# One-hot forms stored once and loaded again, and the count stretch's keys made four columns at a time, in a four-layer graph network

## The chip, the cores and the metric

The kernel runs on one core of one Trainium2 chip. The time is device microseconds of one execution. Before the change it is 6291.43 us, the median of 14 executions (6259.13 to 6341.54).

The core's engines are named as in the profile: PE is TensorE (its weight loads are a row of their own, PEld), DVE is VectorE, ACT is ScalarE, POOL is GpSimd, SP is SyncE, which here issues most of the DMAs. Each engine works through its own instructions in order.

## What is computed

A graph of N = 3125 nodes with 128 features and E = 100,000 edges (`src`, `dst`, sorted by `dst`) goes through four residual blocks, each before a layer norm and a ReLU:

```python
edge_index = jnp.stack([src, dst])
h = jnp.maximum(_layernorm(x, axis=-1), 0.0)
x = x + _L0_gnn_ref(h, edge_index, ...)      # 3 attention layers, one head, with self loops
h = jnp.maximum(_layernorm(x, axis=-1), 0.0)
x = x + _L1_gnn_ref(h, edge_index, edge_attr_64, ...)   # messages by a 3-layer MLP per edge
h = jnp.maximum(_layernorm(x, axis=-1), 0.0)
x = x + _L2_gnn_ref(h, edge_index, ...)      # 2 attention layers with 4 heads
h = jnp.maximum(_layernorm(x, axis=-1), 0.0)
x = x + _L3_gnn_ref(h, edge_index, edge_weight, ...)    # 2 graph convolutions
```

The several-headed layer, which the change touches most, is

```python
e = jax.nn.leaky_relu(xl[src] + xr[dst], NEG)
score = jnp.einsum('ehd,hd->eh', e, att)
m = jax.ops.segment_max(score, dst, num_segments=N)
ex = jnp.exp(score - m[dst])
den = jax.ops.segment_sum(ex, dst, num_segments=N)
alpha = ex / (den[dst] + 1e-16)
out = jax.ops.segment_sum(alpha[:, :, None] * xl[src], dst, num_segments=N)
```

## The kernel before

**Tiles.** Nodes lie in 25 tiles of 128. Edges are sorted by destination, so that the edges of a range of destinations are one range of the list. Two plans cut this list (class `Plan`). The plan for counting has 196 windows of 16 destinations (`cw`), each a matrix of 128 edges by k columns: most windows have 3 or 4 columns (68 and 56 windows), 24 have 5, 16 have 6, 8 each have 7, 8 and 11, 2 have 12, and the first six have 59, 25, 20, 17, 15 and 13; 1025 columns in all. The plan for the edge layers has 30 windows (`ew`) of at most 128 destinations, 840 columns ("chunks" of 128 edges) in all. Chunks are handled in groups of up to C = 4: 15, 11, 8, 9, 10, 8, 7, 7, 12, 10, 9, 9, 8, 8, 7, 7, 7, then 6 seven times... down to 2 groups a window, 220 groups in all.

**Stages in order.**
1. *Count stretch* (`count_edges`). For each of the 196 windows, it counts the edges between sources and destinations by matmuls of one-hot matrices: `by_src` (line 1043, through the helper `even`: the low seven bits of the source against 0..127, for 8 columns at once) is the stationary operand and `by_key` (line 1092, the key against 0..399, one column each) the moving one. The sums go to `count` on ACT.
2. *Three one-headed attention layers* on the dense count matrix.
3. *Message layer* (`message_layer`), over the 220 groups. For each: four gathers of table rows by POOL (line 1348, 128 rows each); a DMA `row` (line 1355) that puts the places of the group's 512 edges within their node tile on all partitions; `at` (line 1359), on DVE, is 1 where partition and place agree (bf16, 128x512); `by_feature` (lines 1371 and 1376) sums node part and gathered part in PSUM; after the MLP, `w` (line 1364), on DVE, is the same relation the other way round (float32, edges on partitions, 512 columns), and line 1577 sums messages by node with it.
4. *Two several-headed layers* (`dynamic_attention_layer`), over the same 30 windows and 220 groups each. `scored` makes the gathers, `row`, `at`, `by_feature`, the leaky ReLU (lines 1806 on ACT and 1807 on DVE), and the scores (line 1813). `weighed` finds the maxima of runs (`run_maxima`, scans on DVE) and the exponentials (line 1831). `summed` makes `w` again (line 1364), `msg` (line 1847) and the sums by node (line 1852). The gathered rows stay in one of G2 = 20 buffers `g2` from `scored` until `summed`. A window's sums are run either beside the next but one window's scores ("apart") or within the next window's ("merged"): `apart = steps(i - 1) + steps(i) + steps(i + 1) < G2`.
   Beside these layers runs `adjacency`, which makes the weighted dense adjacency for the last stage: one-hot matrices by `even` and line 1771, matmuls of line 1775 into one PSUM bank `W`, a copy `rows` by ACT (line 1781) and a DMA to `adj` (line 1782), 196 times.
5. *Two convolutions* on the dense adjacency, read back by DMA.

**Order.** The loops are unrolled in Python; a scheduler then places each engine's instructions, so that work of later groups stands ahead of earlier groups' where buffers allow it. The number of buffers of a tile (`bufs`) says how far: `row` 4, `at` 3, `w` 3, `g1` 6 groups. All plain loads and stores (`row`, `er`, `lane`, `pk`, `adj<-rows`, tables) are issued by SP in its one order; a store waits there until its data is made, and what stands behind it waits too. The gathers are issued by POOL.

**Both layers make the same forms again.** `at` and `w` depend on the edges' places alone, not on the layer. Before the change, they are made by DVE three times: in the message layer and in each several-headed layer.

Of the kernel before, what the change touches and what calls it, by code (L numbers as in the profile page):

```python
# [8 lines left out]
F32 = mybir.dt.float32  # L9
# [735 lines left out]
def sorted_path(ctx: ExitStack, tc: tile.TileContext, a: dict, out: bass.AP, flag_out: bass.AP):  # L745
# [23 lines left out]
    def bc(ap, shape):  # L769
        return ap.to_broadcast(shape)  # L770
# [32 lines left out]
                   allow_small_or_imprecise_dtypes=True)  # L803
    iota_by = const.tile([P, P, 8], BF16, name="iota_by")
    nc.vector.tensor_copy(iota_by, bc(iota_row[:, :, None], [P, P, 8]))
    weights = []

    def load_matrix(name, src):
# [231 lines left out]
    def even(out_t, a_t, row, j0, n, op):  # L1040

        n += n % 2
        nc.vector.tensor_tensor(out_t[:, :, :n], a_t[:, :, :n], bc(row[:, None, j0:j0 + n], [P, P, n]), op)  # L1043

    def count_edges(count):

        with tc.tile_pool(name="f_cw", bufs=2) as wp:
            tail0 = plan.nw * NW
            nc.vector.memset(count[:, :, tail0:], 0)
            many = wp.tile([P, plan.nw], F32, name="many", bufs=1)  # L1050
            below_255 = wp.tile([P, 1], F32, name="below_255", bufs=1)
            nc.vector.memset(below_255, -254.0)
            for w0, w1, c0, cols in plan.batches:
                code = wp.tile([P, cols, 2], I32, name="code", bufs=1)
                own = wp.tile([P, cols], F32, name="own", bufs=1)
                for w, col, k in plan.cw[w0:w1]:
                    r = at_register(base_c, w, P * k)
                    reads.append(nc.sync.dma_start(
                        code[:, col - c0:col - c0 + k, :],
                        codes[bass.ds(r, P * k), :].rearrange("(p k) i -> p k i", p=P)))  # L1060
                    nc.gpsimd.memset(own[:, col - c0:col - c0 + k + k % 2], float(w))
                    if k % 2:
                        nc.gpsimd.memset(code[:, col - c0 + k:col - c0 + k + 1, :], 0)
                ti = wp.tile([P, cols], I32, name="ti", bufs=1)
                tf = wp.tile([P, cols], F32, name="tf", bufs=1)
                keep = wp.tile([P, 3, cols], F32, name="keep", bufs=2)
                key = keep[:, 0, :]
                low = wp.tile([P, cols], BF16, name="low", bufs=2)
                code_i = code[:, :, 0]

                nc.vector.tensor_scalar(ti, code_i, 16, None, ALU.logical_shift_right)
                nc.vector.tensor_tensor(own, ti, own, ALU.not_equal)
                nc.vector.tensor_scalar(ti, code_i, 127, None, ALU.bitwise_and)
                nc.vector.scalar_tensor_tensor(keep[:, 1, :], own, FAR, ti, ALU.mult, ALU.add)
                nc.vector.tensor_copy(low, keep[:, 1, :])

                nc.vector.tensor_scalar(ti, code_i, 12, NW - 1, ALU.logical_shift_right, ALU.bitwise_and)
                nc.vector.tensor_copy(tf, ti)
                nc.vector.tensor_scalar(ti, code_i, 7, 31, ALU.logical_shift_right, ALU.bitwise_and)
                nc.vector.scalar_tensor_tensor(key, ti, float(NW), tf, ALU.mult, ALU.add)  # L1080
                nc.scalar.copy(keep[:, 2, :], code[:, :, 1].bitcast(F32))
                nc.sync.dma_start(kept[:, :, c0:c0 + cols], keep)
                for w, col, k in plan.cw[w0:w1]:
                    pt = bank("ABC"[w % 3])
                    for k0 in range(0, k, 8):
                        kn = min(8, k - k0)
                        j0 = col - c0 + k0
                        by_src = wp.tile([P, P, 8], BF16, name="by_src", bufs=3)
                        even(by_src, iota_by, low, j0, kn, ALU.is_equal)
                        for i in range(kn):  # L1090
                            by_key = wp.tile([P, n_key], BF16, name="by_key", bufs=6)
                            nc.vector.tensor_scalar(by_key, iota_key, key[:, j0 + i:j0 + i + 1], None,  # L1092
                                                    ALU.is_equal)
                            nc.tensor.matmul(pt[:, :n_key], by_src[:, :, i], by_key,  # L1094
                                             start=(k0 + i == 0), stop=(k0 + i == k - 1))
                    nc.scalar.copy(count[:, :, w * NW:(w + 1) * NW],
                                   pt[:, :n_key].rearrange("p (t d) -> p t d", d=NW))
                    junk = wp.tile([P, n_key], BF16, name="junk")
                    nc.scalar.activation(junk, pt[:, :n_key], AF.Relu, bias=below_255,
                                         accum_out=many[:, w:w + 1])  # L1100
            worst = wp.tile([P, 1], F32, name="worst", bufs=1)
            nc.vector.tensor_reduce(worst, many, AX.X, ALU.add)
            pt = bank("D")
            nc.tensor.matmul(pt[:1, :1], worst, ones[:, 0:1], start=True, stop=True)
            nc.vector.tensor_copy(flags[:, 3:4], pt[:1, :1])
            load_edge_windows(wp)
            for t in range(NT):
                own_t = count[:, t, t * P:(t + 1) * P]
                nc.vector.tensor_add(own_t, own_t, ident)
# [236 lines left out]
    def gather(tab, g, j0, c0, n):  # L1346
        for c in reversed(range(n)):
            nc.gpsimd.indirect_dma_start(  # L1348
                out=g[:, j0 + c, :], out_offset=None, in_=tab,
                in_offset=bass.IndirectOffsetOnAxis(ap=src_i[:, c0 + c:c0 + c + 1], axis=0))  # L1350

    def node_by_slot(c0, n):

        row = wk.tile([P, SL], BF16, name="row", bufs=4)
        nc.sync.dma_start(row[:, :n * P], bass.AP(tensor=place_d.tensor,
                                                  offset=place_d.offset + c0 * P,
                                                  ap=[[0, P], [1, n * P]]))
        at = wk.tile([P, SL], BF16, name="at", bufs=3)
        nc.vector.tensor_scalar(at[:, :n * P], row[:, :n * P], pidx, None, ALU.is_equal)  # L1359
        return at  # L1360

    def slot_by_node(c0, n):
        w = wk.tile([P, C, P], F32, name="w", bufs=3)
        nc.vector.tensor_tensor(w[:, :n, :], bc(iota_row[:, None, :], [P, n, P]),  # L1364
                                bc(dst_l[:, c0:c0 + n, None], [P, n, P]), ALU.is_equal)
        return w

    def by_feature(pt, R3, t, at, g, j0, n, more=None):
# [371 lines left out]
    def adjacency(pool):  # L1740
        for t in range(NT):
# [16 lines left out]
            for w, col, k in ws:  # L1758
                sums = bank("W")
                for k0 in range(0, k, C):  # L1760
                    kn = min(C, k - k0)
                    j0 = col - c0 + k0
                    by_src = pool.tile([P, P, C], BF16, name="by_src")
                    even(by_src, iota_by, low, j0, kn, ALU.is_equal)
                    by_wgt = [pool.tile([P, P, C], BF16, name=f"by_wgt{q}") for q in range(3)]
                    for q, part in enumerate((w1, w2, w3)):
                        even(by_wgt[q], by_src, part, j0, kn, ALU.mult)
                    yield
                    by_key = pool.tile([P, C, n_key], BF16, name="by_key")
                    for i in reversed(range(kn)):  # L1770
                        nc.vector.tensor_scalar(by_key[:, i, :], iota_key, pk[:, 0, j0 + i:j0 + i + 1],  # L1771
                                                None, ALU.is_equal)
                    for i in range(kn):
                        for q in range(3):
                            nc.tensor.matmul(sums[:, :n_key], by_wgt[q][:, :, i], by_key[:, i, :],  # L1775
                                             start=(k0 + i + q == 0),
                                             stop=(k0 + i == k - 1 and q == 2))
                    if k0 + kn < k:
                        yield
                rows = pool.tile([P, n_key], F32, name="rows")  # L1780
                nc.scalar.copy(rows, sums[:, :n_key])
                nc.sync.dma_start(adj[t, :, w % per, :], rows)
                yield

    most_cols = max(sum(c[2] + c[2] % 2 for c in plan.cw if c[0] // per == t) for t in range(NT))

    G2 = 20


    def dynamic_attention_layer(i_layer, R3, T3, beside):  # L1790
# [3 lines left out]
        def scored(i, S, gs):  # L1794

            _, _, t, w0, k = plan.ew[i]
            for c0, n in chunks_of(w0, k):
# [1 line left out]
                g = gp.tile([P, C, D], F32, name="g2", bufs=G2)  # L1799
                gs.append(g)  # L1800
                gather(tab, g, 0, c0, n)
                at = node_by_slot(c0, n)
                y1 = bank("A")
                by_feature(y1, R3, t, at, g, 0, n)
                low_y = wk.tile([P, SL], F32, name="low_y", bufs=3)
# [28 lines left out]
        def summed(i, exs, gs):  # L1834
# [6 lines left out]
            for c0, n in chunks_of(w0, k):  # L1841
# [1 line left out]

                msg = wk.tile([P, C * HEADS, HW], F32, name="msg", bufs=3)
                e = ex[:, j0:j0 + n, :].rearrange("p c h -> p (c h)")
                w = slot_by_node(c0, n)
                nc.vector.tensor_mul(msg[:, :n * HEADS, :HD],  # L1847
                                     gs[j0 // C][:, :n, :].rearrange("p c (h d) -> p (c h) d", d=HD),
                                     bc(e[:, :, None], [P, n * HEADS, HD]))
# [171 lines left out]
```

## Time and profile before

| what | value |
|---|---|
| median of 14 executions | 6291.43 us |
| profiled execution, its own time | 6316.27 us |
| its span | 6314.4 us |
| PE busy | 4691.3 us (74%) |
| PE weight loads busy | 3855.0 us (61%) |
| DVE busy | 3396.1 us (54%) |
| ACT busy | 1743.5 us (28%) |
| POOL busy | 2562.6 us (41%) |
| mean granted PE clock | 0.84 |
| moved by DMA | 423.25 MB, 67 GB/s over the span |
| queue of SP's and ACT's DMAs (q1) | 248.15 MB, 13.5% of 16 engines |
| queue of POOL's gathers (q0) | 166.13 MB, 10.7% of 16 engines |

The operations that the change touches, each as a group of the profile:

| line, engine | what | count | busy us | mean ns |
|---|---|---|---|---|
| 1092 DVE | `by_key` of the count stretch, 128x400 | 1025 | 260.1 | 317 |
| 1094 PE | count matmuls, 128x400 | 1025 | 97.7 + 84.6 + 83.7 | 356, 347, 355 |
| 1359 DVE | `at`, 128x512 bf16 | 660 | 230.0 | 349 |
| 1364 DVE | `w`, 128x512 float32 | 660 | 434.9 | 660 |
| 1348 POOL | gathers | 2520 | 2532.8 | 1005 |
| 1781 ACT | `rows` | 196 | 96.4 | 492 |

How to read it: a group's busy time is the union of its instructions' spans, its mean is that of one. Instructions of one engine overlap in the profile by a few tens of nanoseconds and more, so the time that one takes from its engine's stream is read from start to start on the timeline. "Idle before, released by" names the engine whose semaphore came last before the instruction; "issue" is a wait that no semaphore in the profile explains. Some matmul records are missing from a trace.

### The profile page before, as it was taken

The page shows a single profiled execution, that of the slowest core. Times are in us where ns is not written, and L with a number is a line of the kernel's source. Part 1 is how long each engine was busy: PE and PEld are TensorE (multiplying, and loading weights), DVE is VectorE, ACT ScalarE, POOL GpSimd, SP SyncE. Part 2 cuts the span into 40 slices and gives each one's busy share as a digit, 9 for nine tenths or more (in the row PEclk, how much of TensorE's full clock was granted, in tenths as well). Part 3 has the DMA queues.
Part 4 walks back from the last instruction along what each step waited for, and adds up shares of the span by engine and source line. Part 5 has one row for each costly group of instructions (what it writes and reads, how often), then busy time and mean ns, then how long its engine had stood idle before and what let it go on. Part 6 is the DMA issues. An engine that isn't in the chain of part 4 may idle for free. (4 is left out here: it accounts for less than half of the span.)

```text
span 6314.4 us, 85314 instructions
## 1 busy us (share of the span) xinstructions
PE 4691.3 (74%) x30043; PEld 3855.0 (61%) x30361; DVE 3396.1 (54%) x9835; ACT 1743.5 (28%) x4234; POOL 2562.6 (41%) x3155
## 2 busy tenths in 40 slices
PE   4769995878887886567687767874576777677798
PEld 2339984767776775346465656663465555566698
DVE  7998885333334445345455546572354555566633
ACT  1578884222222232111111112121111212122211
POOL 1000001656666563454544445634645454455200
PEclk9989996889999997778787778886787888788899
DMA  1010002333333331122222222221222222222266
GB/s 47 7 22 1 2 1 52 80 82 85 78 86 82 80 82 50 42 53 53 55 57 60 57 59 65 67 55 50 62 67 64 70 70 68 70 74 73 86 250 219
DMA packets 299197, 423.25 MB, mean 67 GB/s; under 512 B 113380, under 2 KB 243090, under 8 KB 292614
## 3 DMA queue, kind: packets, MB, share of 16 engines
q1 hardware_dynamic: 215589, 248.15, 13.5%
q0 software_dynamic: 80800, 166.13, 10.7%
q8 instruction: 241, 3.95, 0.3%
q10 hardware_dynamic: 2368, 3.40, 0.2%
q14 instruction: 199, 1.62, 0.1%
HBM read 367.97 MB, written 49.45 MB: 66 GB/s over the span
## 5 line engine op out<-in xcount | busy, mean ns | idle before, releaser
L1348 POOL DMA_INDIRECT g<-tab,src_i x2520 | 2532.8, 1005 | 3140.3 <-issue 967.7
L1364 DVE TENSOR_TENSOR w<-iota_row,dst_l 128x512 f32<-128x512 f32 (+2 forms) x660 | 434.9, 660 | 854.0 <-remote 271.3
L1775 PE MATMUL W<-by_key,by_wgt 128*128 128x400 bf16 x3075 | 705.1, 376 | 193.8 <-issue 105.0
L1852 PE MATMUL C<-msg,w 128*128 128x132 f32 x3360 | 570.6, 313 | 178.6 <-issue 155.5
L1807 DVE TENSOR_TENSOR low_y<-A,low_y 128x512 f32<-128x512 f32 (+3 forms) x440 | 291.0, 661 | 748.6 <-ACT low_y L1806 416.0
L1376 PEld LDWEIGHTS A<-ident,g 128*128 128x128 f32 x3360 | 502.7, 210 | 293.1 <-issue 220.4
L1376 PE MATMUL A<-ident,g 128*128 128x128 f32 x3360 | 529.8, 295 | 196.7 <-issue 175.9
L1813 PE MATMUL sp<-att_h,low_y 128*128 128x4 f32 x3360 | 463.2, 257 | 262.0 <-issue 144.6
L1813 PEld LDWEIGHTS sp<-att_h,low_y 128*128 128x128 f32 x3360 | 470.3, 212 | 283.0 <-issue 152.4
L1775 PEld LDWEIGHTS <-by_wgt 128*128 128x128 bf16 x3075 | 365.1, 123 | 434.7 <-issue 302.2
L1852 PEld LDWEIGHTS C<-msg,w 128*128 128x128 f32 x3360 | 489.1, 216 | 207.6 <-issue 187.6
L1806 ACT ACTIVATE low_y<-A 128x512 f32<-128x512 f32 (+3 forms) x440 | 254.2, 578 | 1197.8 <-PE A L1376 658.8
L1371 PE MATMUL A<-at,R 128*128 128x512 bf16 (+3 forms) x1108 | 370.3, 402 | 91.3 <-issue 60.8
L1043 DVE TENSOR_TENSOR by_wgt<-by_src,w 128x512 bf16<-128x512 bf16 (+1 forms) x918 | 329.1, 396 | 168.8 <-remote 85.5
L1630 PE MATMUL B<-ets,w1c 128*128 128x256 f32 (+1 forms) x868 | 266.1, 434 | 157.1 <-DVE ets L1619 95.5
L1371 PEld LDWEIGHTS <-R 128*128 128x128 bf16 x1980 | 201.0, 105 | 222.7 <-issue 117.4
L1359 DVE TENSOR_SCALAR at<-row,pidx 128x512 bf16<-128x512 bf16 (+2 forms) x660 | 230.0, 349 | 172.5 <-remote 78.8
L1577 PE MATMUL C<-x,w 128*128 128x130 f32 x1680 | 257.4, 293 | 68.9 <-ACT x L1569 62.9
L1636 ACT ACTIVATE x<-B,mb 128x512 f32<-128x512 f32 (+1 forms) x220 | 146.7, 667 | 572.1 <-PE B L1376 302.7
L1771 DVE TENSOR_SCALAR by_key<-iota_key,pk 128x400 bf16<-128x400 f16 x1025 | 287.1, 323 | 30.8 <-PE A L1376 14.6
L1094 PEld LDWEIGHTS <-by_src 128*128 128x128 bf16 x1025 | 134.0, 149 | 273.6 <-DVE by_key L1092 158.2
L1847 DVE TENSOR_TENSOR msg<-g,ex 128x512 f32<-128x512 f32 (+3 forms) x440 | 286.8, 659 | 7.8 <-ACT ex L1831 5.3
(404 smaller groups left out, 7670.3 us busy)
## 6 DMA issues: line engine op xcount, KB each, us to landing
A<-adj SPq DMA_DIRECT2D x48, 1600.0 KB
row<-place_d SPq DMA_DIRECT2D x597, 128.0 KB
g<-tab,src_i POOLq DMA_INDIRECT x2520
adj<-rows SPq DMA_DIRECT2D x196, 200.0 KB
er<-in_edge_attr_dram SPq DMA_DIRECT2D x39, 512.0 KB
tab<-T SPq DMA_DIRECT2D x21, 192.0 KB
row<-place_d SPq DMA_DIRECT2D x24, 96.0 KB
A<-adj SPq DMA_DIRECT2D x2, 800.0 KB
```

Source lines behind the costliest of these rows:

```text
L1043: nc.vector.tensor_tensor(out_t[:, :, :n], a_t[:, :, :n], bc(row[:, None, j0:j0 + n], [P, P, n]), op)
L1348: nc.gpsimd.indirect_dma_start(out=g[:, j0 + c, :], out_offset=None, in_=tab, in_offset=bass.IndirectOffsetOnAxis(ap=src_i[:, c0 + c:c0 + ...
L1364: nc.vector.tensor_tensor(w[:, :n, :], bc(iota_row[:, None, :], [P, n, P]), bc(dst_l[:, c0:c0 + n, None], [P, n, P]), ALU.is_equal)
L1371: nc.tensor.matmul(pt[:, :n * P], R3[i][:, t * D:(t + 1) * D], at[:, :n * P], start=(i == 0), stop=False, skip_group_check=True)
L1376: nc.tensor.matmul(pt[:, c * P:(c + 1) * P], g[:, j0 + c, :], ident, start=False, stop=(c == n - 1), skip_group_check=True)
L1630: nc.tensor.matmul(p3[:, c:n:2, :], W1c[:, c, :], ets[:, :m * P].rearrange("p (c e) -> p c e", e=P), start=False, stop=False, skip_group_c ...
L1771: nc.vector.tensor_scalar(by_key[:, i, :], iota_key, pk[:, 0, j0 + i:j0 + i + 1], None, ALU.is_equal)
L1775: nc.tensor.matmul(sums[:, :n_key], by_wgt[q][:, :, i], by_key[:, i, :], start=(k0 + i + q == 0), stop=(k0 + i == k - 1 and q == 2))
L1807: nc.vector.tensor_max(low_y[:, :n * P], y1[:, :n * P], low_y[:, :n * P])
L1813: nc.tensor.matmul(sp[:, c * HEADS:(c + 1) * HEADS], low_y[:, c * P:(c + 1) * P], att_h, start=True, stop=True)
L1847: nc.vector.tensor_mul(msg[:, :n * HEADS, :HD], gs[j0 // C][:, :n, :].rearrange("p c (h d) -> p (c h) d", d=HD), bc(e[:, :, None], [P, n * ...
L1852: nc.tensor.matmul(acc[:, :AW], w[:, c, :], msg[:, c * HEADS:(c + 1) * HEADS, :].rearrange("p h d -> p (h d)"), start=(i == first_of[t] an ...
```

## The change

Three things change.

*Count stretch.* Four columns' keys are made by one tensor_tensor of 128 x 400 x 4 through the helper `even`, against an iota repeated four times (`iota_kby`, a new constant) and an f16 copy of the keys (`key16`, made by ACT once for each of the four batches). `even` rounds an odd number of columns up to the next even one. The matmuls read their moving operand with a step of four elements.

```diff
+    iota_kby = const.tile([P, NT * NW, C], F16, name="iota_kby")
+    nc.vector.tensor_copy(iota_kby, bc(iota_key[:, :, None], [P, NT * NW, C]))
...
-        nc.vector.tensor_tensor(out_t[:, :, :n], a_t[:, :, :n], bc(row[:, None, j0:j0 + n], [P, P, n]), op)
+        nc.vector.tensor_tensor(out_t[:, :, :n], a_t[:, :, :n],
+                                bc(row[:, None, j0:j0 + n], [P, a_t.shape[1], n]), op)
...
+                key16 = wp.tile([P, cols], F16, name="key16", bufs=2)
+                nc.scalar.copy(key16, key)
...
-                        for i in range(kn):
-                            by_key = wp.tile([P, n_key], BF16, name="by_key", bufs=6)
-                            nc.vector.tensor_scalar(by_key, iota_key, key[:, j0 + i:j0 + i + 1], None,
-                                                    ALU.is_equal)
-                            nc.tensor.matmul(pt[:, :n_key], by_src[:, :, i], by_key,
-                                             start=(k0 + i == 0), stop=(k0 + i == k - 1))
+                        for i0 in range(0, kn, C):
+                            by_key = wp.tile([P, n_key, C], BF16, name="by_key", bufs=3)
+                            even(by_key, iota_kby, key16, j0 + i0, min(C, kn - i0), ALU.is_equal)
+                            for i in range(i0, min(i0 + C, kn)):
+                                nc.tensor.matmul(pt[:, :n_key], by_src[:, :, i], by_key[:, :, i - i0],
+                                                 start=(k0 + i == 0), stop=(k0 + i == k - 1))
```

*One-hot forms.* The message layer still makes `at` and `w` on DVE, and now also stores each to DRAM. The several-headed layers load them instead of loading `row` and making them: one load of up to 128 KB for `at`, one of up to 256 KB for `w` a group, all issued by SP.

```diff
+    at_d = dram.tile([-(-KT // C) + NE, P, SL], BF16, name="at_d")
+    at_row = {}
+
+    def node_by_slot_again(c0, n):
+        at = wk.tile([P, SL], BF16, name="at", bufs=5)
+        nc.sync.dma_start(at[:, :n * P], at_d[at_row[c0], :, :n * P])
+        return at
...
         nc.vector.tensor_scalar(at[:, :n * P], row[:, :n * P], pidx, None, ALU.is_equal)
+        at_row[c0] = len(at_row)
+        nc.sync.dma_start(at_d[at_row[c0], :, :n * P], at[:, :n * P])
         return at
+
+    w_d = dram.tile([-(-KT // C) + NE, P, C * P], F32, name="w_d")
+
+    def slot_by_node_again(c0, n):
+        w = wk.tile([P, C, P], F32, name="w", bufs=4)
+        nc.sync.dma_start(w[:, :n, :].rearrange("p c d -> p (c d)"), w_d[at_row[c0], :, :n * P])
+        return w
...
+        nc.sync.dma_start(w_d[at_row[c0], :, :n * P], w[:, :n, :].rearrange("p c d -> p (c d)"))
         return w
...
-                at = node_by_slot(c0, n)
+                at = node_by_slot_again(c0, n)
...
-                w = slot_by_node(c0, n)
+                w = slot_by_node_again(c0, n)
```

*Buffers.* `rows` of `adjacency` has one buffer instead of two, and G2 is 19 instead of 20.

```diff
-                rows = pool.tile([P, n_key], F32, name="rows")
+                rows = pool.tile([P, n_key], F32, name="rows", bufs=1)
...
-    G2 = 20
+    G2 = 19
```

## The prediction

> **What bounds the kernel now.** I read first the stretches of the span by stage, since an average over the span mixes four limits. Columns: length of the stretch, then busy time and number of instructions of PE, weight load, DVE, ACT and POOL, then granted clock, DMA share and GB/s.
>
> ```profile
> 60.00:440.00 380.00, 268.97 (x1050) 137.94 (x1050) 369.21 (x1309) 212.56 (x593) 9.38 (x280) 0.96 0.08 11
> ...
> 1010.00:2500.00 1490.00, 1151.99 (x7339) 997.24 (x7446) 582.51 (x1719) 415.54 (x1027) 827.95 (x840) 0.88 0.30 78
> 2490.00:4230.00 1740.00, 1257.80 (x7562) 985.62 (x7668) 929.30 (x2747) 281.93 (x900) 845.41 (x840) 0.79 0.22 57
> 4230.00:5970.00 1740.00, 1210.28 (x7379) 959.51 (x7486) 925.30 (x2835) 330.38 (x1071) 859.40 (x840) 0.78 0.25 65
> ```
>
> The count stretch (first row) is DVE's: 369 of 380 us. In the message layer (second row) and in the two several-headed layers (last two) PE is the busiest by far, and DVE has about half of its time free.
>
> Then two short stretches inside the first several-headed layer:
>
> ```profile
> 2635.00:2665.00 30.00, 29.68 (x216) 23.77 (x219) 23.12 (x70) 6.13 (x16) 0.00 (x0) 1.00 0.12 32
> 3005.00:3032.00 27.00, 9.38 (x23) 3.76 (x23) 1.78 (x4) 0.60 (x1) 17.98 (x20) 0.56 0.22 56
> ```
>
> When the layer runs well, PE is full (29.68 of 30 us) with DVE at 77%. When it runs badly, PE makes 23 matmuls in 27 us, while POOL issues gather after gather; DVE has worked 1.78 us and cannot be what is late. Third, the waits of PE's weight loads over both several-headed layers (us in total, times, longest):
>
> ```profile
> PEld L1775 <- issue: 302.2, 636, 33.4
> PEld A L1376 <- issue: 220.4, 213, 3.2
> PEld C L1852 <- issue: 187.6, 226, 3.2
> PEld sp L1813 <- issue: 152.4, 104, 31.9
> PEld sp L1813 <- DVE low_y L1807: 120.2, 40, 31.2
> PEld L1371 <- issue: 114.8, 202, 5.6
> PEld E L1719 <- DVE F L1711: 28.4, 13, 12.8
> ...
> PEld L1775 <- DVE by_key L1771: 19.2, 8, 10.5
> ...
> PEld L1371 <- DVE at L1359: 7.3, 5, 3.6
> ```
>
> Five rows of "issue" come to 977 us: no wait for any engine. DVE's four rows come to 175 us. So what a lighter DVE can win is bounded by 175 us, not by the DVE time saved.
>
> **The count stretch's keys.** Now each column of edges costs one tensor_scalar of 128x400, and four at once would be one tensor_tensor of 128x1600. Starts on DVE's timeline give the rates:
>
> ```profile
> 200.90 0.67 DVE L1043 TENSOR_TENSOR by_src<-iota_by,low 128x1024 bf16<-128x1024 bf16 x1
> 201.50 1.71 DVE L1092 TENSOR_SCALAR by_key<-iota_key,keep 128x400 bf16<-128x400 f16 x7
> 203.14 0.67 DVE L1043 TENSOR_TENSOR by_src<-iota_by,low 128x1024 bf16<-128x1024 bf16 x1
> ...
> 426.22 0.42 DVE L1043 TENSOR_TENSOR by_src<-iota_by,low 128x512 bf16<-128x512 bf16 x1
> 426.56 0.78 DVE L1092 TENSOR_SCALAR by_key<-iota_key,keep 128x400 bf16<-128x400 f16 x3
> ```
>
> Seven keys take 203.14 - 201.50 = 1.64 us, 0.234 each; 1025 columns make 240 us. The tensor_tensor of line 1043 occupies 0.60 us for 1024 elements and 0.34 for 512, so 0.13 per 256, and 1600 would take 0.89 and 800 (two columns) 0.49. By the plan, windows of 3, 4, 5, 6, 7, 8 columns and the long ones give 263 groups of four and 43 of two, an odd three being rounded up to four: 263 x 0.89 + 43 x 0.49 = 255 us. That is **+15 us**: a full four wins 0.05, but the 68 windows of three lose 0.19 each. The wide iota copy is one instruction (the 1024-element one took 0.67, so 1.0), and the f16 copy of the keys on ACT (0.53 us by the copy beside it, line 1081) now stands before each of the four batches' first key; behind it DVE waits, PE behind DVE: +2. PE then reads its moving operand with a step of four. No row shows that; the nearest are bf16 weight loads, 105 ns packed (line 1371), 149 with a step of eight (line 1094). At that ratio 1025 matmuls of line 1775's pitch (0.18 us) cost 262 us, still under DVE's 369, so nothing. **Sum +18**, from 0 (the keys' rate for wide ones ten per cent better) to +40.
>
> [...]
>
> **The message layer.** Each of 220 groups now also stores its two one-hot forms: 32 KB and 64 KB a chunk, 840 chunks, 83 MB. SP's queue moved 248.15 MB in 13.5% of sixteen engines' 6314 us, 18.2 GB/s an engine, so this is 284 us of all sixteen, and the DMA share goes from 0.30 to about 0.49; the gathers share them, six groups ahead. On SP the store of `at` waits for DVE line 1359 and that of `w` for line 1364; behind them stand the next `row` load, `er`, and the table's stores, and for a late row waits DVE, then PE. Cover is the four `row` buffers: SP is already held by line 1359 now. The new slot waits (DVE's fourth `at` or `w` waits for a landing) are three groups of 6.8 us away. I take **+10**; bounds 0 and 220 x 0.32 us (one SP issue exposed each) = +70.
>
> **The several-headed layers.** DVE loses `at` (349 ns) and `w` (659 ns) of 440 groups: 154 + 290 = 444 of its 1855 us, 24%. If PE's 175 us of waiting for DVE shrink in proportion, **-42**; bounds 0 (they belong to the slow stretches) and -175. The `at` load has the bytes of the `row` load that it replaces and lands straight in the tile; `w` adds 110 MB, by the same rate 378 us of sixteen engines in 3480, share up by 0.11, with room.
>
> G2 falls to 19, and the test "sum of three windows' steps < G2" flips for one window a layer (7 + 6 + 6 = 19): it then runs merged. From the trace's starts of line 1831, windows 12 to 16 of the first layer, merged, took 8.56 us a step and 17 to 20, apart, 6.9. Two windows of six steps x 1.66 = **+20**, from 0 to +40.
>
> Queues: before, `row` was four groups ahead and `at` three more. Now `at` is five and `w` four ahead, and both stand in SP's order behind the store of `rows`, for which SP waits 618 us in 96 times. `rows` itself has one buffer: ACT's next copy waits for the landing of the last (about 3.0 us by `pk`, issued at 3036.71 and used at 3039.70), with 196 of them 17.8 us apart. PE waits for line 1781 for 71.8 us now; I take a quarter more, **+17**, bounds 0 and +100.
>
> **Sum:** 18 + 10 - 42 + 20 + 17 = +23. The profiled execution took 6316.3 us (span 6314.4), 24.8 above the median of 6291.4; so 6339 for a like execution, **6314 us** for the median. What separates this kernel from no change is about 0.3%, 19 us.
>
> **Rivals.**
> 1. *PE gets DVE's time back* (faster). All 175 us of waits go, because the in-order DVE queue (by_wgt and by_key ahead of low_y) was late, not slow PE: 18 + 10 - 175 + 20 + 17 = -110, **6181**. For it: low_y's row is the largest wait with a named engine. Against: longest 31 us, as long as the slow stretches. It decides from 65 us of recovered waits. 0.33.
> 2. *Loads come late.* `at` and `w` behind the `rows` store: if a third of the 96 waits exposes a landing of 3.0 us, +96 in place of the 17: **6393**. For it: longest such wait 64.9 us, more than four groups of 7.9. Against: SP issues in 0.32 us. 0.23.
> 3. *The message layer's rows are no longer ahead*: the queue is in strict step with the stores, and each group pays a landing: 220 x 3.0 = 660 in place of the 10, **6964**. Against: SP is held by the same DVE line already. 0.04.
> 4. The forecast, small on either side of its sum (own range 6270 to 6360): 0.40.
>
> **How the numbers follow.** The forecast's 0.40 is 0.22 slower by over 19 us, 0.14 within it, 0.04 faster. With the rivals: faster 0.37, same 0.14, slower 0.49. The range reaches from 6180 (rival 1) to 6430 (rival 2 and some of its bound), leaving out rival 3 and the tails.
>
> **What would show it.** Line 1092's successor near 0.89 us, and a count stretch some 18 us longer; in the message layer the same 6.8 us a group with DMA share near 0.49; in the several-headed layers DVE's 929 us down to about 705, with PE's "issue" waits where they were. Wrong if those "issue" waits themselves move by more than a tenth (98 us): nothing in the profile says what makes them, except that gathers run back to back then, and this change moves when gathers may start.

## The result, and the profile after

| | kernel before | changed kernel |
|---|---|---|
| median | 6296.19 us (47 executions) | 6379.4 us (10 executions) |
| lowest to highest | 6259.13 to 6343.08 | 6331.19 to 6406.77 |
| span of the profiled execution | 6314.4 us | 6374.6 us |

The ratio is 1.0125, with a 95% interval from 1.0101 to 1.0149: the change makes the kernel slower by 83 us. The prediction was 6314 us, 23 above the median that it started from, with a range from 6180 to 6430.

The stretches of the changed kernel by stage, in the columns of the prediction's first view (length, busy time and number of PE, weight load, DVE, ACT and POOL, granted clock, DMA share, GB/s): the count stretch, the message layer, the two several-headed layers.

```profile
60.00:484.00 424.00, 386.11 (x1050) 146.41 (x1050) 394.87 (x592) 217.70 (x597) 9.52 (x296) 0.96 0.08 10
1054.00:2534.00 1480.00, 1151.56 (x7357) 996.78 (x7464) 582.53 (x1719) 417.04 (x1031) 830.55 (x843) 0.89 0.48 135
2534.00:4274.00 1740.00, 1243.27 (x7567) 984.17 (x7669) 756.93 (x2301) 282.87 (x889) 819.84 (x837) 0.78 0.31 88
4274.00:6014.00 1740.00, 1205.66 (x7295) 940.02 (x7396) 727.26 (x2280) 325.65 (x1040) 829.40 (x840) 0.78 0.33 95
```

The count stretch is 44 us longer (380 before, 424 now), and PE, which was busy for 269 us of it, is busy for 386. The message layer moves 135 GB/s in place of 78 in the same time. In the several-headed layers DVE has given up 929 - 757 = 172 and 925 - 727 = 198 us, and the layers are no shorter for it (the rows are cut to equal lengths; from the first gather to the convolution it is 3515 us, 3484 before).

The waits of PE's weight loads in those two layers (us in total, times, longest):

```profile
PEld L1798 <- issue: 339.4, 564, 24.7
PEld A L1399 <- issue: 269.8, 250, 3.2
PEld C L1875 <- issue: 216.9, 242, 3.9
PEld sp L1836 <- issue: 214.4, 166, 30.5
PEld L1394 <- issue: 121.0, 223, 2.7
PEld sp L1836 <- DVE low_y L1830: 49.0, 15, 20.7
...
PEld L1798 <- DVE by_key L1794: 14.6, 3, 10.5
```

The wait for `low_y` has gone from 120.2 to 49.0 us, and the five rows of "issue", 977 us before, now come to 1162. How much two traces of the same layers differ is seen in e1 below: its several-headed layers are those of the kernel before, with as much work for DVE and PE's instructions in the same order (DVE's differ in places). Its five rows of "issue" come to 1022 us, and its row of `low_y` is

```profile
PEld sp L1818 <- DVE low_y L1812: 55.3, 35, 13.6
```

So the growth of "issue" is more than that difference, and the fall of the wait for `low_y` is not: it cannot be put to the lighter DVE.

This is how such a wait looks inside. PE's timeline in the first several-headed layer (start, duration, instruction, idle time before it), and GpSimd's at the same time:

```profile
3040.48 0.27 PE L1875 MATMUL C<-msg,w 128*128 128x132 f32 x1 [1.63 <-issue]
3041.22 0.38 PE L1875 MATMUL C<-msg,w 128*128 128x132 f32 x1 [0.47 <-issue]
3041.95 0.38 PE L1875 MATMUL C<-msg,w 128*128 128x132 f32 x1 [0.35 <-issue]
...
3048.35 0.38 PE L1875 MATMUL C<-msg,w 128*128 128x132 f32 x1 [0.84 <-issue]
3050.43 0.38 PE L1875 MATMUL C<-msg,w 128*128 128x132 f32 x1 [1.71 <-issue]
```

```profile
3040.19 0.94 POOL L1353 DMA_INDIRECT g<-tab,src_i  x1 [0.30 <-issue]
3041.44 0.94 POOL L1353 DMA_INDIRECT g<-tab,src_i  x1 [0.30 <-issue]
3042.68 0.94 POOL L1353 DMA_INDIRECT g<-tab,src_i  x1 [0.30 <-issue]
```

Matmuls start about 0.7 us apart or at multiples of that, with no semaphore to wait for that the profile shows, and GpSimd issues a gather every 1.25 us. Below, starts of PE (matmuls or weight loads) less than 0.3 us after the first of a group count as one. A **slow stretch** is five or more such starts in a row, 0.62 to 0.80 or 1.25 to 1.55 us apart, up to the end of the last. A **long run** is 17 or more gathers each less than 1.6 us after the last. From the first gather of the several-headed layers to the convolution, the kernel before has 692 us of slow stretches and 665 of 1680 gathers in long runs; the changed kernel has 946 us and 912 gathers. e1, with the same layers as before, has 616 and 649, so a difference of some 80 us is no finding. (The recorded expectations count a little differently: 695 us for the kernel before, 978 for the changed one, 944 in e2, 564 in e4.) The two don't coincide: in the kernel before, 360 of the 692 us lie within long runs, which fill 843 of these 3484 us.

### The profile page after: what moved, and what is told of

Same layout as the page of the kernel before. It is cut to its first block, busy times and chain, and to the rows that moved or that the text cites. A ratio compares the mean times of both kernels' runs of the same rounds, so it can differ in the third digit from the quotient of the medians.

```text
span 6374.6 us, 85932 instructions
## 1 busy us (share of the span) xinstructions
PE 4802.0 (75%) x30049; PEld 3853.0 (60%) x30361; DVE 3075.5 (48%) x8237; ACT 1758.1 (28%) x4238; POOL 2509.1 (39%) x3155
## 5 line engine op out<-in xcount | busy, mean ns | idle before, releaser
L1353 POOL DMA_INDIRECT g<-tab,src_i x2520 | 2479.8, 984 | 3234.0 <-ACT R L1328 851.9
L1399 PE MATMUL A<-ident,g 128*128 128x128 f32 x3360 | 545.2, 298 | 246.0 <-issue 218.8
L1394 PE MATMUL A<-at,R 128*128 128x512 bf16 (+2 forms) x1114 | 380.9, 407 | 85.0 <-issue 69.4
L1386 DVE TENSOR_TENSOR w<-iota_row,dst_l 128x512 f32<-128x512 f32 (+1 forms) x220 | 146.6, 666 | 557.9 <-PE C L1600 219.7
L1394 PEld LDWEIGHTS <-R 128*128 128x128 bf16 x1980 | 202.4, 105 | 216.4 <-issue 123.2
L1587 PE MATMUL D<-mw,x 128*128 128x128 f32 x1680 | 251.4, 285 | 71.1 <-ACT x L1659 38.1
```

The source lines that it names most:

```text
L1353: nc.gpsimd.indirect_dma_start(out=g[:, j0 + c, :], out_offset=None, in_=tab, in_offset=bass.IndirectOffsetOnAxis(ap=src_i[:, c0 + c:c0 + ...
L1394: nc.tensor.matmul(pt[:, :n * P], R3[i][:, t * D:(t + 1) * D], at[:, :n * P], start=(i == 0), stop=False, skip_group_check=True)
L1399: nc.tensor.matmul(pt[:, c * P:(c + 1) * P], g[:, j0 + c, :], ident, start=False, stop=(c == n - 1), skip_group_check=True)
```

## The experiments

Each run is beside runs of the kernel before on the same chip, and the chips turned out to differ: the kernel before took 6290 us (chip A: e1 to e4), 4952 us (chip B: e5 to e8), 6237 us (chip C: e9, e10) and 6295 us (chip D: e11, e12). Only ratios go from one chip to another, and not all of those: the kernel of e5 has 1.0859 on chip B and, run again as e10, 0.9529 on chip C.

### The three parts alone (chip A)

**e1**, the count stretch's keys, with the wide iota in the count's own pool, so that no buffer is lost:

```diff
+            iota_kby = wp.tile([P, NT * NW, C], F16, name="iota_kby", bufs=1)
...
+                            even(by_key, iota_kby, key16, j0 + i0, min(C, kn - i0), ALU.is_equal)
```

> Only the count stretch's keys are changed (the wide iota lies in the count's own pool, so the several-headed layers keep 20 gather buffers and two rows buffers). Theory: the matmuls that read every fourth element of the wide key set the pace, 0.37 us each where the old ones came 0.23 to 0.25 us apart, so the count stretch is 44 us longer and the whole kernel about 6340 against 6296. Rival (the prediction's term): the strided operand is hidden, DVE still sets the pace, +18 us, 6314. A third: the stretch is longer but later stages absorb part of it, under +10.

Measured: 6333.3 us, ratio 1.0074 (1.0043 to 1.0106), +43 us by the medians; the stretch from the first to the last count matmul, by the starts of their weight loads, is 420.8 us where it was 377.3.

**e2**, the stores and loads of `at` and `w` alone:

```diff
-                at = node_by_slot(c0, n)
+                at = node_by_slot_again(c0, n)
...
-                w = slot_by_node(c0, n)
+                w = slot_by_node_again(c0, n)
```

> Only the one-hot forms are stored and loaded (20 gather buffers, two rows buffers, old keys). Theory: in the several-headed layers the waits for DVE go (about -100 us) but the waits for nothing that the profile shows grow by about as much, because gathers then run back to back more often; the total moves by less than 40 us, 6260 to 6330. Rival 1: the relief arrives, about 6190. Rival 2: the loads themselves are late (the share of DMA engines 0.30 in place of 0.22), 6360 or more.

Measured: 6307.9 us, ratio 1.0035 (1.0005 to 1.0066), +17 us. Slow stretches 962 us, 929 gathers in long runs. In its trace the waits of PE's weight loads for DVE, all rows from 2430 to 6030 us, come to 111 us where the kernel before has 202, and those for "issue" to 1137 where it has 1029. By the time, both rivals are out. The waits look like the theory's, but e1's trace, without any loads, has 121 and 1074: the waits for DVE are as low there, so which wait the 17 us come from is not shown.

**e3**, the two smaller buffers alone:

```diff
-                rows = pool.tile([P, n_key], F32, name="rows")
+                rows = pool.tile([P, n_key], F32, name="rows", bufs=1)
...
-    G2 = 20
+    G2 = 19
```

> Only 19 gather buffers and one rows buffer, all else as before. Theory: window 17 of each layer runs merged with its neighbours, 16 and 23 us over windows 16 to 18 of the two layers in the changed kernel's trace, so +35 to +45 us, about 6336; rows adds under 10. Rival: the lost buffers cost no more than 10 us and the several-headed layers' loss comes from the loads.

Measured: 6314.0 us, ratio 1.0041 (1.0015 to 1.0067), +24 us. Window 17 takes 59.3 and 62.8 us in the two layers where it took 46.1 and 46.4.

The three come to 43 + 17 + 24 = 84 us; the change measured 83. Each has an interval of 16 to 20 us either way, so agreement to 1 us is luck; that they add up within these intervals is shown, and e9 below says the same. Whether the 24 us belong to the gather buffers or to `rows` was not split.

### Why the keys cost more than the sum had it (chip B)

**e8** keeps the wide key and lets each matmul read 400 elements that lie side by side, so that the counts mix the keys of four columns (one execution):

```diff
-                                nc.tensor.matmul(pt[:, :n_key], by_src[:, :, i], by_key[:, :, i - i0],
+                                nc.tensor.matmul(pt[:, :n_key], by_src[:, :, i], by_key[:, (i - i0) * n_key:(i - i0 + 1) * n_key],
```

> As e1, but each matmul reads 400 keys that lie side by side in the wide tile in place of every fourth one: the counts then mix the keys of four columns, which is all that is left out. Theory (the moving operand's step of four sets the pace): the count stretch falls back from 421 us to 378 plus about 18, its matmuls come 0.25 us apart. Rival (DVE's wide operation or the waits between the two engines set the pace): it stays at 415 to 425 us.

Measured: first to last count matmul 399.3 us (377.3 before, 420.8 in e1). The count stretch can be compared across chips: the kernel of e5, with the old keys, takes 378.1 us there and that of e6, with the new ones, 421.4. PE's timeline in the changed kernel, then in e8:

```profile
199.54 1.99 PE L1099 MATMUL A<-by_key,by_src 128*128 128x400 bf16 x5
201.35 3.05 PE L1099 MATMUL B<-by_key,by_src 128*128 128x400 bf16 x8
```

```profile
200.94 1.85 PE L1101 MATMUL A<-by_key,by_src 128*128 128x400 bf16 x7
203.34 0.90 PE L1101 MATMUL B<-by_key,by_src 128*128 128x400 bf16 x4 [0.56 <-ACT count L1103]
```

Eight matmuls run together for 3.05 us with the step of four; packed, seven take 1.85. With the step, 934 of the 1024 distances between starts of matmuls lie between 0.34 and 0.39 us, with a median of 0.36. Packed, half of them (505) lie between 0.16 and 0.18 us, and PE waits for keys in between (154 us in all at its weight loads). On DVE, the changed kernel's timeline shows who waits for whom:

```profile
201.63 0.98 DVE L1045 TENSOR_TENSOR by_key<-iota_kby,key 128x1600 bf16<-128x1600 f16 x1
203.00 0.99 DVE L1045 TENSOR_TENSOR by_key<-iota_kby,key 128x1600 bf16<-128x1600 f16 x1 [0.39 <-PE B L1099]
203.91 0.68 DVE L1045 TENSOR_TENSOR by_src<-iota_by,low 128x1024 bf16<-128x1024 bf16 x1
```

DVE now idles 0.39 us for PE to free a key buffer (13 us in all). The wide operation takes 203.91 - 203.00 = 0.91 us of DVE's stream, as the sum had it (0.89). So of the 44 us, 22 stay when the step is taken away (the sum's +18), and 22 are the moving operand's step, which the sum had hidden. Of the 22 that stay, 6 stand at the start: the first matmul comes 15.0 us after the first weight load in e8, 9.0 before, where the sum had 1 + 2. The step of four is not free here: matmuls start 0.36 us apart with it (the median) and half of them 0.16 to 0.18 us apart packed, and on chip B the stretch takes 421.4 us with it (e6) against 399.3 (e8).

### Pacing the gathers

**e4** puts one GpSimd instruction, which reads a score written four groups earlier, ahead of each group's gathers:

```diff
+                if len(asked) >= 4:
+                    S0, j1 = asked[-4]
+                    nc.gpsimd.tensor_scalar(pace, S0[:, 0, 1 + j1:2 + j1], 1.0, None, ALU.mult)
+                asked.append((S, j0))
                 gather(tab, g, 0, c0, n)
```

> The kernel before, with one small GpSimd instruction ahead of each group's gathers in the several-headed layers that reads a score written four groups earlier, so that gathers come four at a time, spread over PE's work, in place of runs of 16 and more. Theory: a long run of gathers is what makes PE issue once per 0.70 us; 695 us of such stretches at 29.5 us per 256 instructions in place of 18 cost about 270 us, so 6030, within 100. Rival: PE's slow issue has another cause and the gathers only run together because PE is slow then: within 0.5% of 6296, the slow stretches as long as before, or slower by the gathers' lost lead.

Measured on chip A: 6154.3 us, ratio 0.9791 (0.9745 to 0.9838). The slow stretches fell to 552 us only, and 525 gathers are still in long runs. The edit did less than it says: no data ties the gathers to the new instruction, and in the trace up to 17 gathers follow one of them, eight or more in 88 places.

**e5** ties them, by writing into the gather's own buffer:

```diff
-                    nc.gpsimd.tensor_scalar(pace, S0[:, 0, 1 + j1:2 + j1], 1.0, None, ALU.mult)
+                    nc.gpsimd.tensor_scalar(g[:, :n, 0], S0[:, :n, 1 + j1], 1.0, None, ALU.mult)
```

> As e4, but the small GpSimd instruction writes into the gather buffer itself, so every gather of a group stands behind it; in e4 the order on GpSimd's queue still let 8 to 12 gathers follow one of them. Theory (long runs of gathers slow PE's issue): the stretches in which PE issues once per 0.70 us fall from e4's 564 us to under 300, and the time from 6154 to about 6050. Rival: e4's gain is only the start of each layer (its 79 gathers in a row) and a little luck, so 6150 again. Second rival: gathers held back so strictly come late, PE waits for them (41.7 us for A in e4, then over 150), 6200 and more.

**e6** is the same in the changed kernel.

> The changed kernel with the same pacing. Theory (the loads' relief was eaten by longer runs of gathers: 978 us of slow stretches against 695): pacing wins more here than in the kernel before, at least 200 us, about 6130 against 6379, and the rest over e5 is the count stretch's 44 us and the merged windows. Rival (the relief was worth nothing in itself, since DVE was never what PE waited for): it wins the same as e5, so e5 plus about 80.

Both fell on chip B: ratios 1.0859 (1.0837 to 1.088) and 1.0725 (1.0701 to 1.075). The times that were expected for chip A don't apply, because chip B has no slow stretches to remove; of the mechanisms only e5's second rival shows: PE waits 459 us at line 1376, the transposes of the gathered rows (a row of "issue" again; that it is the gathers it waits for is a reading). e8's trace, whose several-headed layers are those of the kernel before, shows them there (the two layers, then the largest wait):

```profile
2140.00:3340.00 1200.00, 1090.05 (x7542) 878.81 (x7541) 920.46 (x2732) 292.67 (x900) 887.04 (x827) 0.93 0.31 81
3340.00:4600.00 1260.00, 1130.24 (x7716) 916.86 (x7715) 949.56 (x2863) 343.51 (x1087) 950.25 (x868) 0.93 0.34 92
```

```profile
PEld A L1383 <- DMA g<-tab,src_i: 250.3, 173, 5.3
```

From the first gather of these layers to the convolution the same work takes 2432 us in place of 3484, at a clock of 0.93 in place of 0.78, with 681 gathers in long runs and not one slow stretch; PE then waits for gathers, and holding them back cost 8.6% there. Between e5 and e6, on one chip, the changed kernel is 58 us faster although its count stretch is 43 longer, so the loads and the buffers together win some 100 us there. By what is not shown: the waits of PE's weight loads for DVE in these layers come to 28 us in e5 and 19 in e6, and e6 even has 642 gathers in long runs where e5 has 261.

**e7** replaces the gathers of the several-headed layers by plain loads, and leaves out the selection of rows by edge (one execution):

```diff
-                gather(tab, g, 0, c0, n)
+                for c in reversed(range(n)):
+                    nc.sync.dma_start(g[:, c, :], tab[c * P:(c + 1) * P, :])
```

> The kernel before with the gathers of the several-headed layers replaced by plain loads of the first rows of the table, as many and of the same size, on SyncE's queue: the selection of rows by edge is left out. Theory (it is GpSimd's back-to-back indirect transfers that slow PE's issue): the stretches of 0.70 us per instruction are all but gone in both layers, under 100 us. Rival (it is the landing of the same bytes, or PE's own instruction supply): they stay at 500 to 700 us.

Measured on chip B: 4629.8 us (4952 before), no slow stretch. As no trace taken on that chip has any, this tells nothing of their cause.

**e10** is the kernel of e5 again, on chip C:

> The kernel of e5, because e5 ran on a chip that takes 4952 us for the kernel before and shows no slow stretches at all, with gathers 40 and more in a row. Theory 1 (long runs of gathers make a held-back PE slow): on a chip that takes 6290 us, the slow stretches fall from 695 us to under 300 and the time is under 6154, e4's. Theory 2 (the slow stretches are a state of PE on that chip which no order of the gathers takes away; e4's gain is the start of each layer): slow stretches over 450 us and a time of 6100 to 6400, since gathers that start late cost there too. On the faster chip it repeats e5, ratio 1.086.

Measured: 5945.5 us, ratio 0.9529 (0.9489 to 0.9569). Slow stretches 90 us, 128 gathers in long runs. The two layers, and PE's two largest waits there:

```profile
2410.00:3980.00 1570.00, 1276.04 (x7699) 1001.43 (x7700) 935.70 (x2796) 294.44 (x922) 956.00 (x1040) 0.84 0.25 63
3980.00:5600.00 1620.00, 1298.03 (x7730) 1023.74 (x7728) 959.83 (x2917) 342.52 (x1109) 992.00 (x1079) 0.82 0.28 71
```

```profile
PEld A L1376 <- issue: 385.5, 250, 7.6
PEld L1775 <- issue: 146.5, 586, 4.7
```

Theory 2 is out: with the long runs went the slow stretches (e9, on the same chip, has 816 us), and the layers are shorter although PE now waits longer at the transposes of the gathered rows (385.5 us, 220.4 before). That the length of the runs is the cause, as theory 1 has it, is not shown by this alone, since pacing also changes when every gather is made.

**e11** adds the loads of e2 to it, on chip D:

> The one-hot forms loaded as in e2 and the gathers paced as in e10; old count keys, 20 gather buffers, two rows buffers. Theory (the relief of DVE is real, and in e2 it was spent on longer runs of gathers and slow stretches: 944 us against 695): once the runs are broken up it pays. On a chip that takes about 6250 us for the kernel before, e10's ratio of 0.953 falls by another 1 to 2% (e6 won 58 us over e5 although it also paid 44 us for the keys), so 0.935 to 0.943. Rival (PE was never late for DVE there; e2's loss is the loads' own): 0.953 or more. On a chip of 4950 us: about 100 us under e5's 5377, ratio 1.06 to 1.07.

Measured: 5937.1 us, ratio 0.9432 (0.9394 to 0.9469); slow stretches 69 us, 75 gathers in long runs. Without pacing the loads cost 0.35%; with it they win 1.0% between e10 and e11 by the ratios, but by the times, 5945 and 5937 us, next to nothing. The two ran on different chips, so a gain on the slower chips is not shown; nor do the waits for DVE show one (128 us in e10, 161 in e11, from 2500 to 5900 us). Only e5 and e6 show a gain on one chip. This is the fastest version found against its own chip's runs of the kernel before, but e5 and e6 say what pacing would do on chip B.

**e12** lets the gathers wait for the score of six groups earlier:

```diff
-                if len(asked) >= 4:
-                    S0, j1 = asked[-4]
+                if len(asked) >= 6:
+                    S0, j1 = asked[-6]
```

> As e11, but a group's gathers wait for the score of six groups earlier in place of four. Theory: what pacing costs where PE isn't held back is gathers that come late (PE waits 385 us for them at line 1376 in e5); two more groups of lead give most of that back on a chip of 4950 us: ratio 1.00 to 1.03. On a chip of 6250 us the runs become longer again: between e11 and e4 (0.935 to 0.979). Rival: the lead isn't what costs (the extra GpSimd instruction and its order are), so the same as e11 on either chip.

Measured: 6490.1 us, ratio 1.0308 (1.0268 to 1.0348), outside every expectation. GpSimd's timeline in its trace says why:

```profile
2906.29 1.74 POOL L1822 TENSOR_SCALAR g<-S 128x4 f32<-128x4 f32 x6 [15.01 <-DVE S L1755]
2908.19 1.25 POOL L1348 DMA_INDIRECT g<-tab,src_i  x1 [0.16 <-POOL g L1822]
2909.74 1.18 POOL L1348 DMA_INDIRECT g<-tab,src_i  x1 [0.30 <-issue]
...
2938.87 0.95 POOL L1348 DMA_INDIRECT g<-tab,src_i  x1 [0.30 <-issue]
2939.84 0.24 POOL L1822 TENSOR_SCALAR g<-S 128x4 f32<-128x4 f32 x1
```

Here, as in other places, six groups' waiting instructions stand together ahead of their 24 gathers. So the first gather waits for what the sixth instruction waits for, and then all run together: 977 gathers in long runs (the longest has 28; 79 in the kernel before), slow stretches 451 us, and PE waits longest at the transposes of the gathered rows:

```profile
PEld A L1394 <- issue: 523.8, 293, 8.1
```

So it is no test of more lead. Against e11 on the same chip it shows the long runs and the slow stretches coming back together, but not in step: the kernel before has more slow stretches (692 us) with fewer gathers in long runs (665).

### The change with its buffers given back (chip C)

**e9** is the changed kernel with the wide iota in the count's pool, 20 gather buffers and two `rows` buffers.

> The whole change with its two lost buffers given back: the wide iota lies in the count's own pool, so the several-headed layers have 20 gather buffers and two rows buffers again. Theory: the change's cost is the sum of three parts that don't touch each other (keys +43 us in e1, buffers +24 in e3, loads +17 in e2), so without the buffers' part the kernel is 0.4% nearer to the kernel before: ratio 1.008 to 1.011 on a chip that runs the kernel before in about 6290 us. Where the kernel before takes about 4950 us (a chip that grants PE more), the several-headed layers go as fast as 840 gathers at 1.29 us allow and PE waits for gathers, so DVE's relief is worth under 20 us there too, the keys cost their 44 us, and the ratio is 1.005 to 1.011. Rival: the loads' relief of DVE pays where PE isn't held back, ratio 1.000 or less there.

Measured: 6309.2 us, ratio 1.0111 (1.0082 to 1.0139): e1 and e2 multiplied give 1.0109. Slow stretches 816 us, 842 gathers in long runs.

## Why the prediction came out as it did

| term | predicted | measured alone |
|---|---|---|
| count stretch's keys | +18 us | +43 (e1; 27 to 67) |
| stores and loads of the one-hot forms | +10 - 42 = -32 | +17 (e2; 3 to 42) |
| 19 gather buffers, one `rows` buffer, loads behind it | +20 + 17 = +37 | +24 (e3; 9 to 42) |
| sum | +23 | +84; the change itself +83 |

The direction and the range held; the sum was 60 us short. Two of its terms were too low, by 25 and 49 us; that a third was too high, by 13, brought it nearer, which is luck.

**The keys.** DVE's part was right: 0.91 us for a wide operation, and 22 us more in all without the step (e8) against 18. The step "At that ratio 1025 matmuls of line 1775's pitch (0.18 us) cost 262 us, still under DVE's 369, so nothing" failed. A packed weight load against a strided one, 105 to 149 ns, was the nearest row, but it is another operation: the matmuls started every 0.36 us with the step and as often as every 0.17 us packed, where the working had 0.18 x 149 / 105 = 0.26. 1025 x 0.36 = 369 us of PE, as much as DVE had before; with three key buffers between them each now waits for the other (in the changed kernel's trace DVE 13 us for PE to free a key buffer, PE's weight loads 61 us for DVE's keys). The upper bound of +40 did not take PE in.

**The message layer.** The +10 was not seen. From the first to the last matmul of its sums (line 1577, now 1600) it takes 1339 us (1346 before), and the DMA share of 0.48 is the 0.49 of the working. Rival 3 is out.

**The several-headed layers.** DVE's busy time fell to 757 and 727 us (about 705 was expected). The step that failed is the -42, which let PE's waits for DVE shrink with DVE's work and the time with the waits: with the stores' +10 it gave -32, and e2 measured +17. The waits for DVE did fall, from 202 us to 83 over both layers, and so rival 1's condition, 65 us of recovered waits, was met. But in e1 they are 121 us with DVE's work in these layers as before, so one trace of each kernel can't tell a recovered wait from such a difference, and both the -42 and rival 1 priced these waits as time. (The layers took 3484 us in the kernel before's trace, 3444 in e1's and 3471 in e2's.) The prediction's own test failed too: the "issue" waits were to stay and to move by no more than 98 us; they moved by 185 (44 in e1, 113 in e2). The working had named what would move them ("this change moves when gathers may start") and given it no price. What that price is stays open: from the first gather to the convolution slow stretches grew by 946 - 692 = 254 us, and the time by 3515 - 3484 = 31, less than e1's trace differs.

A possible chain is this: `msg` and `low_y` are no longer behind `at` and `w` on DVE's queue, gather buffers come free closer together, and GpSimd, which waits for them, issues its gathers in longer runs. The traces, one of each kernel, show that with the loads more gathers are in long runs (842 to 929 in e9, the changed kernel and e2; 649 to 740 in e1, the kernel before and e3) and that slow stretches are longer (816 to 962 us against 616 to 704). The runs show that pacing takes both away and 4.7% of the time on chip C. Not shown is that the earlier freeing of buffers lengthens the runs, that long runs are what slows PE (e12 has 977 gathers in them and 451 us; chip B 681 and 642, in e8 and e6, and no slow stretch), and that the slow stretches are what the loads' gain was spent on.

**The buffers.** Right in kind: window 17 runs merged. In the changed kernel windows 16 to 18 take 16 and 23 us longer in the two layers, so +20 was low there; in e3, where the loads are left out, 5 and 6, so it was high.

**`rows` and the order on SP.** The +17 and rival 2 were wrong in sign. The loads were hardly ever late: PE's only waits for them that the profile names are 0.7 us for `at` and 0.5 for `w`. SP waits less for `rows`, 216.4 us in place of 618.4 (208 in e2, with the loads alone; 570 in e3, with the buffers alone), probably since its queue is now held at the loads' own buffers first (in the changed kernel's trace the `at` load waits 420.7 us for the transposes of line 1399, the `w` load 381.3 us for the sums of line 1875). PE's 71.8 us of waiting for ACT's `rows` are down to 1.9. The waits on SP and PE's for the load:

```profile
SPq L1805 <- ACT rows L1804: 216.4, 100, 9.2
```

```profile
PEld C L1875 <- DMA at<-at_d: 0.7, 2, 0.4
```

**What stays open.** Why PE issues so slowly beside gathers on chips A, C and D, and not on chip B, no run here shows; whether the indirect form, the bytes that land or PE's supply of instructions sets it off is open too, since e7 ran on chip B. No lateness shows in that supply: of the 241 transfers of 16 KB that the profile calls instruction (queue q8), those in these layers take 0.99 us by the median in the kernel before, the longest 1.78, and 1.00 on chip B in e8. How the change stands without pacing on chip B was not tried.

## What to carry to other kernels

Before a wait is priced as time, read it in a second trace of the same code: here the waits for one engine went from 202 to 121 us in layers whose work had not changed. Where the unexplained waits beside it are five times as large and go with another queue's bursts, ask what the relieved engine lets that queue do, and price it. Before an operand is laid out for the convenience of its producer, price its reader with that step by a measurement of the same operation: here a ratio of weight loads gave 0.26 us a matmul, and 0.36 was measured. Tie a pacing instruction by data to what it is to hold back: in e4, where nothing tied the gathers to it, up to 17 followed one; look at the built queue, and at a second chip, before trusting its gain.

## What was not expected of the hardware

One program on one core took 4952 us on one chip and 6237 to 6295 us on three others, with granted clocks of 0.94 and 0.84. The convolution, beside which nothing is gathered, took 331 us on chips A and B alike, and the count stretch 377 and 378. The difference lies in the layers that gather: the message layer took 1346 us in the kernel before and 1069 in e5, and the several-headed layers 3484 and, in e8, 2432. In the changed kernel's trace the granted clock is 0.52 in the stretch from 3040 to 3065 us, where PE makes 22 matmuls in 25 us:

```profile
3040.00:3065.00 25.00, 8.55 (x22) 4.54 (x22) 2.74 (x8) 0.44 (x1) 16.52 (x17) 0.52 0.23 65
```

There, PE's starts are 0.7 us apart from 3036.3 us on, and the clock falls from 1.0 to 0.5 at 3040.9, with the starts as far apart after as before. Of the 101 slow stretches of that kernel, 48 begin at full clock, which falls 0.9 to 5.5 us later; 53 begin while it is still low. In those 48 the slow issue comes first and the low clock after it, so there the low clock doesn't explain the slow issue. PE isn't idle in the stretch above: it is busy for 8.55 of the 25 us, and no two of its starts, weight loads included, lie more than 1.5 us apart. What makes the clock fall no run here shows.
